# Two adaLN layers on one core: the first square weights are fetched inside layer 1's timetable, in the room of the softmax weights, and the tile for unread products has one buffer

## The chip, the core and the metric

The kernel runs on one core of a Trainium2 chip. A core has five engines with their own instruction streams: TensorE (PE in the profile; PEld is its weight load), VectorE (DVE), ScalarE (ACT), GpSimd (POOL) and SyncE (SP), which here only issues transfers. GpSimd issues transfers too. The engines wait for one another by semaphores. The metric is the time of one execution on the device, in microseconds; each figure is the median of several.

## The reference

Eight images of 512 tokens with 256 features pass through two layers. Each layer adds a modulated attention and a modulated feed-forward to its input (`ga`, `gb`, `ca`, ... come from a small product of a conditioning vector):

```python
def two_layers(x):
    h = _layernorm(x) * (1 + ca) + sa                  # layer 0
    x = x + ga * attn0(h)
    h = _layernorm(x) * (1 + cb) + sb
    x = x + gb * ffn0(h)
    h = _layernorm(x) * (1 + ca) + sa                  # layer 1, with its own mod
    x = x + ga * attn1(h)
    h = _layernorm(x) * (1 + cb) + sb
    return x + gb * ffn1(h)

def attn0(x):   # rmsnorm, 16 heads of 16; linear attention and a window of 64 tokens, side by side
    lin = linear_attention_causal(taylor_feature_map(q @ Wqf), taylor_feature_map(k @ Wkf), v)
    win = sliding_window_attention(q, k, v)
    return x + concatenate([lin, win]) @ Wout

def attn1(x):   # 16 heads of 16, rotary, causal softmax
    attn = softmax(where(causal, Q @ K.T * scale, NEG_INF))
    return (attn @ V) @ w_proj + b_proj

def ffn1(x):    # ternary weights times a scale per output; hidden width 1024
    h = silu(tlin(x, w1_w, w1_s)) * tlin(x, w2_w, w2_s)
    h = gelu(tlin(h, h1_w, h1_s), approximate=False)
    h = gelu(tlin(h, h2_w, h2_s), approximate=False)
    return tlin(h, w3_w, w3_s)
```

## The kernel before

**Layers 0 and 1 by a timetable.** Everything up to the first gates of layer 1's feed-forward is written as small functions that are put into one list `plan` with a time in steps: `when(t, f)` for layer 0, `when1(t, f)` for layer 1. The list is sorted by time, and the functions are called in that order under a manual schedule, so each engine's instructions stand in just this order. Layer 1's attention takes six steps for each of 32 units (an image, a half of the heads, one of two head sets), and layer 1's steps begin while layer 0 still runs.

**Maxima.** Both softmaxes subtract a maximum per query row. `scores` (layer 1) and `win_scores` (layer 0) multiply queries and keys into PSUM, and a `post` function runs a VectorE `tensor_tensor_reduce` over each block: it adds a mask, takes the minimum of the negated values, and leaves one number per row in `maxima` (L1128, L524). The instruction also writes its elementwise product. Nobody reads this: it goes to a tile `junk`, 512 bf16 wide, tagged `junk` with two buffers. The sums of squares of layer 0's norm (`squares`, L375) use the same tile. On VectorE each of these is two instructions: the reduction itself and a reading of the accumulator, which writes `maxima`. The transposes L538 (layer 0) then bring the maxima to the rows of the queries, where L544 adds them. L1225 transposes layer 1's result back to tokens, in a PSUM tag with two buffers (`mm`) that the projection out, whose sum with `x` is L1277, uses too.

**Room.** SBUF is given out in stacks from the left and from the right. On the left stand the pools `w0`, `tok0`, `fm0` and `at0`, opened in this order in one `lctx` that is closed at the end of the timetable. `at0` holds the softmax weights: the tag of each bank has 4, 3 or 2 buffers. Its last reader is the product `values` (L1209) of the last unit. On the right stand the feed-forward's weights `ffn_w` and, from step 187 on (`room`), its gates' parts `ffn_g`.

**The first gates.** Layer 1's feed-forward works on each image with hidden width 1024 in eight column blocks f. All its values are held as a high and a low part in a 32-bit format that TensorE takes faster (`split`: a VectorE cast L195 makes the high part, and L196 the low one, on GpSimd where `rest` says so). The first image's gates are part of the timetable: `gated(f)` at steps 200.0, 200.6, 203.7, 209.6, 211.0, 214.0, 215.0 and 216.0 multiplies (L1377), `gate_parts` follows with the Silu (L1389), the product (L1392, into `row`, a tag `flat` of two buffers) and the split, whose low part is GpSimd's for the first seven.

**The feed-forward.** After the timetable a flag is loaded on every engine, and a branch (L1547) takes one of two versions. The one that runs here, `feed_forward(True)`, opens its pools where `lctx` had been, in the order `h2`, `g2`, `tok2`, `hw`, `mm2`. Its first transfers on GpSimd's queue are the eight slices (512 KB each) of the first square matrix `h1T`, then eight of the second, `h2T`, then `w3T`. Inside the branch, instructions are ordered by a scheduler. The first square product is `times("h1T", ...)`, L1466, with row L1512 on ScalarE (Gelu) and a split; the second is the same line with L1518.

Of the kernel before, what the change touches and what calls it, by code (L numbers as in the profile page):

```python
# [8 lines left out]
FP = mybir.dt.float32  # L9
BF = mybir.dt.bfloat16  # L10
# [14 lines left out]
NF = DH // P  # L25
WIN = 64
BIG = 3.0e38
PAD = (24, 32)

# [5 lines left out]
def adaln_two_layers_kernel(ctx: ExitStack, tc: tile.TileContext, t, out):  # L37
# [163 lines left out]
    with ExitStack() as lctx:  # L201
        wp = lctx.enter_context(tc.tile_pool(name="w0", bufs=1))
        tok = lctx.enter_context(tc.tile_pool(name="tok0", bufs=1))
        fm = lctx.enter_context(tc.tile_pool(name="fm0", bufs=1))
        atp = lctx.enter_context(tc.tile_pool(name="at0", bufs=2))
        sc = lctx.enter_context(tc.tile_pool(name="sc0", bufs=3, space=PSUM))
        mm = lctx.enter_context(tc.tile_pool(name="mm0", bufs=2, space=PSUM))
        only0 = ExitStack()
# [74 lines left out]
        def when1(time, what):  # L283
            slow = min(max(time, 0.0), END1)
            plan.append((20 * B + 0.6 + slow + STEP1 * (time - slow), len(plan), what))
# [49 lines left out]
        def prepare(b):  # L335
# [35 lines left out]
            def squares(j):  # L371
                if j == 0:
                    rms["ss"] = tok.tile([P, NTB], FP, name="ss", tag="ss", bufs=2)
                junk = tok.tile([P, T], BF, name="junk", tag="junk", bufs=2)[:, :D]
                nc.vector.tensor_tensor_reduce(  # L375
                    junk, ln["x"][:, j, :], ln["x"][:, j, :], 1.0 / D, 0.0, ALU.mult, ALU.add, rms["ss"][:, j : j + 1]
                )
# [124 lines left out]
        def win_scores(m, h, p, ps):  # L502

            q, k = ready[m // 2, m % 2, "q"], ready[m // 2, m % 2, "k"]
            mats, posts = [], []
            for ii in range(4):
                for i in range(2):
                    for e in range(2):
                        r = slice(64 * p + 32 * i, 64 * p + 32 * i + 32)
                        blk = 4 * h + ii  # L510
                        k0 = max(blk - 1, 0) * 64
                        mats.append(
                            lambda i=i, e=e, ii=ii, r=r, blk=blk, k0=k0: nc.tensor.matmul(  # L513
                                ps[64 * e : 64 * e + 64, i, ii * P : (ii + 1) * P],
                                q[r, e, 64 * blk : 64 * blk + 64], k[r, e, k0 : k0 + P],
                                start=True, stop=True,
                            )
                        )
                for i in range(2):

                    def post(i=i, ii=ii, blk=4 * h + ii):
                        junk = tok.tile([P, T], BF, name="junk", tag="junk", bufs=2)[:, :P]
                        col = 64 * p + 32 * i + 16
                        nc.vector.tensor_tensor_reduce(  # L524
                            junk, ps[:, i, ii * P : (ii + 1) * P], wmask[:, int(blk > 0), :], -1.0, BIG,
                            ALU.add, ALU.min, maxima[:, blk, col : col + 1],
                        )

                    posts.append(post)
            return mats, posts  # L530
# [335 lines left out]
        def bring(i):  # L866
            if i == 0:
                got1["wqkv"] = wp.tile([P, NC, 3 * D], FP, name="wqkv", tag="wqkv")
                nc.sync.dma_start(out=got1["wqkv"], in_=t["L1_attn_w_qkv"].rearrange("(k p) n -> p k n", p=P))
            elif i == 1:  # L870
                got1["rope"] = fm.tile([P, 2, T], FP, name="rope", tag="qm", bufs=2)
                nc.sync.dma_start(out=got1["rope"][:, 0, :], in_=t["rope_cos"])
                nc.sync.dma_start(out=got1["rope"][:, 1, :], in_=t["rope_sin"])
            elif i == 2:


                cmask = got1["cmask"] = fm.tile([P, T], FP, name="cmask", tag="cat0", bufs=2)
                nc.gpsimd.memset(cmask, 0.0)
                diag = cmask[:, T - P : T]
                nc.gpsimd.affine_select(  # L880
                    out=diag, in_=diag, pattern=[[-1, P]], compare_op=ALU.is_ge, fill=-4e9, base=0, channel_multiplier=1
                )
            elif i == 3:

                home = [rp.tile([P, 2, T], FP, name="home", tag="aw", bufs=4) for _ in range(2)]
                got1["wproj"], wps[0] = (home[0][:, i, :].rearrange("p (k n) -> p k n", k=NC) for i in range(2))
                got1["bproj"], got1["bc"] = (home[1][:, 0, i * D : (i + 1) * D] for i in range(2))
                nc.sync.dma_start(out=got1["wproj"], in_=w_proj)
                nc.sync.dma_start(out=got1["bproj"], in_=t["L1_attn_b_proj"].partition_broadcast(P))
                nc.sync.dma_start(out=got1["bc"], in_=mod_dram[0, 4, :].partition_broadcast(P))  # L890
            else:
                only0.close()
                fpool = got1["ffn"] = ctx.enter_context(tc.tile_pool(name="ffn_w", bufs=1, side="right"))
                lp = got1["lp"] = only1.enter_context(tc.tile_pool(name="only1", bufs=1, side="right"))
                got1["wproj"] = load(lp, "wproj", [P, NC, D], w_proj)
                got1["bproj"] = load(lp, "bproj", [P, D], t["L1_attn_b_proj"].partition_broadcast(P))

                for name in ("w1T", "w2T"):
                    full[name] = fpool.tile([P, NC, DH], FR, name=name, tag=name)
                full["h"] = [fpool.tile([P, NC, T], FR, name="h" + e, tag="h" + e) for e in "hl"]  # L900

                fpool.tile([P, PAD[0]], FP, name="pad0", tag="pad0")
                for name in ("w1_s_cols", "w2_s_cols", "h1_s_cols", "h2_s_cols"):
                    full[name] = load(fpool, name, [P, NF], t[name])
                full["w3_s"] = load(fpool, "w3_s", [P, D], t["L1_ffn_w3_s"].partition_broadcast(P))
                full["x0"] = fpool.tile([P, NTB, D], FP, name="x0", tag="x0")
                full["low"] = fpool.tile([P, 22], FP, name="low", tag="low")
                full["flag"] = fpool.tile([1, 1], I32, name="flag", tag="flag")
# [195 lines left out]
        def scores(n, step):  # L1104
# [6 lines left out]
            for qb in ((3,), (2,), (1, 0))[bank]:  # L1111
                m = (qb + 1) * P
                for i, g in enumerate(gs):
# [10 lines left out]

                    def post(i=i, g=g, qb=qb, m=m, o=o):
                        col = 32 * g + 16
                        junk = tok.tile([P, T], BF, name="junk", tag="junk", bufs=2)
                        nc.vector.tensor_tensor_reduce(  # L1128
                            junk[:, :m],
                            ps[:, i, o : o + m],  # L1130
                            got1["cmask"][:, T - m :],
                            -1.0,
                            BIG,
                            ALU.add,
                            ALU.min,
                            maxima[:, NTB * e + qb, col : col + 1],
                        )
# [247 lines left out]
        def gate_parts(f, i):  # L1385
# [4 lines left out]
            else:  # L1390
# [3 lines left out]
                )  # L1394
                split([part[:, f, :] for part in full["g"]], row, nc.gpsimd if f < NF - 1 else None)

        when1(187.0, room)
        for f, at in enumerate((200.0, 200.6, 203.7, 209.6, 211.0, 214.0, 215.0, 216.0)):
            when1(at, lambda f=f: gated(f))
            for i in range(2):  # L1400
                when1(at + (0.3, 0.35)[i], lambda f=f, i=i: gate_parts(f, i))
# [6 lines left out]
    def feed_forward(exact):  # L1408
# [3 lines left out]
        with ExitStack() as fctx:  # L1412
# [3 lines left out]
                w3 = h2p.tile([P, NF, D], FR, name="w3", tag="w3")  # L1416
            gp = fctx.enter_context(tc.tile_pool(name=f"g2{exact}", bufs=1 if exact else 2))
            tok = fctx.enter_context(tc.tile_pool(name=f"tok2{exact}", bufs=2 if exact else 1))
            if exact:
                tok.tile([P, PAD[1]], FP, name="pad1", tag="pad1", bufs=1)  # L1420
            hp = fctx.enter_context(tc.tile_pool(name=f"hw{exact}", bufs=1 if exact else 3))
            mm = fctx.enter_context(tc.tile_pool(name=f"mm2{exact}", bufs=8, space=PSUM))

            if exact:
                h1 = hp.tile([P, NF, DH], FR, name="h1", tag="h1")
                for dst, name in ((h1, "h1T"), (h2, "h2T")):
                    src = t[name].rearrange("(k p) n -> p k n", p=P)
                    for k in range(NF):
                        nc.gpsimd.dma_start(out=dst[:, k, :], in_=src[:, k, :])
                nc.gpsimd.dma_start(out=w3, in_=t["w3T"].rearrange("(k p) n -> p k n", p=P))  # L1430
                full.update(h1T=h1, h2T=h2)

                gs = [full["g"], [gp.tile([P, NF, T], FR, name="g" + e, tag="g" + e) for e in "hl"]]
                xs = [full["x0"], tok.tile([P, NTB, D], FP, name="x1", tag="x1", bufs=1)]
# [184 lines left out]
```

## Time and profile before

| | us |
|---|---|
| median of 3 runs | 1836.17 |
| the runs | 1834.57 to 1839.29 |
| the profiled execution | 1837.94 |
| its span | 1836.2 |
| layer 1's attention at its densest | about 800 to 1155 on the span's scale |
| last product of the timetable's gates (L1377) starts | 1182.60 |
| first product of the square weights (L1466) starts | 1189.72 |

The span is counted from the first to the last instruction of the profiled execution; 1.74 us of that execution lie around it. All places in time below are on the span's scale. In the profile's group lines, the figures behind the bar are busy time, the mean duration of one instruction in ns, and the idle time of the engine in front of the group with what ended most of it. In lines of the timeline they are the start, the duration and, in brackets, idle time before and what ended it. In lines of windows, each engine's busy time with its instructions stands in the order PE, PEld, DVE, ACT, POOL, and then the granted TensorE clock (1.00 is full speed), the share of the DMA engines and GB/s.

### The profile page before, as it was taken

To read this page: it belongs to the slowest core of one execution; us is meant where nothing else is said; L and a number is where in the kernel's file an instruction comes from. 1 tells how busy PE (TensorE), PEld (TensorE's weight loads), DVE (VectorE), ACT (ScalarE), POOL (GpSimd) and SP (SyncE) were. 2 spreads that over 40 slices of the span, in tenths; PEclk is the share of its full clock that TensorE was granted. 3 is DMA by queue.
4 is the path that set the end of the run, shared out by engine and by line. 5 is a ranking of instruction groups with operands and counts; after the bars stand their busy time and mean duration, and the time that the engine had idled before them with its cause. 6 is when DMAs were issued, how large, how long until landed. Compare 5 with 4: busy or idle time off the path is not lost.

```text
span 1836.2 us, 41129 instructions
## 1 busy us (share of the span) xinstructions
PE 1750.3 (95%) x16878; PEld 1196.4 (65%) x16878; DVE 1069.4 (58%) x3708; ACT 887.1 (48%) x1278; POOL 726.3 (40%) x1101
## 2 busy tenths in 40 slices
PE   3999999999999988999999999899999999999998
PEld 2456666666666655455455555588888888888887
DVE  3554665757566466578888887426353554636352
ACT  1675766667666644656666665323131322313221
POOL 4565857667575664357655555400000000000000
PEclk6899999999999999999999999999999999999999
DMA  4100011010100101022221110240000000000000
GB/s 150 45 2 14 5 39 37 5 37 5 40 17 17 57 4 39 1 65 93 72 61 61 62 47 27 100 148 26 1 26 7 21 26 1 27 1 26 1 12 14
DMA packets 41894, 65.98 MB, mean 36 GB/s; under 512 B 4057, under 2 KB 33369, under 8 KB 41697
## 3 DMA queue, kind: packets, MB, share of 16 engines
q1 hardware_dynamic: 36512, 47.02, 8.1%
q0 software_dynamic: 5184, 16.25, 2.9%
q8 instruction: 134, 2.20, 0.5%
q14 instruction: 64, 0.52, 0.1%
HBM read 50.63 MB, written 12.63 MB: 34 GB/s over the span
## 4 chain that ended last, share of the span: by engine, by line
PE 81%; ACT 8%; POOL 5%; issue 2%; DVE 2%; DMA 1%; SPq 0%; POOLq 0%; ACTq 0%; DVEq 0%
PE mm L1466 31%; PE sc L1175 7%; PE mm L717 5%; PE mm L166 4%; PE mm L620 4%; PE sc L480 4%; PE mm L1209 4%; PE mm L1529 3%; PE mm L1027 2%; PE sc L557 2%; PE mm L1267 2%; ACT at L491 2%; PE mm L643 2%; PE mm L1085 2%; PE mm L445 2%
## 5 line engine op out<-in xcount | busy, mean ns | idle before, releaser
L1466 PE MATMUL mm<-gh,h 128*128 128x512 f32 x1024 | 398.8, 391 | 6.7 <-issue 6.7
L1466 PE MATMUL mm<-gl,h 128*128 128x512 f32 x1024 | 398.0, 391 | 0.0
L1128 DVE CUSTOM_DVE_ANT_0 junk<-sc,cmask 128x256 bf16<-128x256 f32 (+3 forms) x512 | 225.0, 486 | 93.2 <-PE sc L1117 92.8
L195 DVE CAST gh<-row 128x512 fp32r<-128x512 f32 x192 | 80.6, 423 | 264.9 <-ACT row L1512 128.9
L1186 ACT ACTIVATE at<-sc 128x768 f32<-128x768 f32 (+1 forms) x192 | 168.7, 881 | 116.0 <-PE sc L1117 102.8
L1466 PEld LDWEIGHTS mm<-gh,h 128*128 128x128 f32 x1024 | 193.3, 189 | 47.3 <-issue 7.1
L1466 PEld LDWEIGHTS mm<-gl,h 128*128 128x128 f32 x1024 | 193.1, 189 | 40.0
L577 POOL TENSOR_SCALAR_AFFINE_SELECT aw<-aw 64x512 f32<-64x512 f32 (+1 forms) x320 | 168.1, 552 | 101.4 <-ACT aw L567 95.5
L491 ACT ACTIVATE at<-sc 128x768 f32<-128x768 f32 (+1 forms) x192 | 164.0, 883 | 68.7 <-PE sc L480 68.0
L1117 PE MATMUL sc<-k,q 32*128 32x512 f32 (+3 forms) x1024 | 192.0, 472 | 3.4 <-ACT at L1186 3.4
L1175 PE MATMUL sc<-qs,k 32*128 32x384 f32 (+3 forms) x1024 | 189.8, 470 | 1.7 <-DVE qs L1159 1.7
L1190 POOL TENSOR_SCALAR_AFFINE_SELECT at<-at 128x256 f32<-128x256 f32 x256 | 103.1, 415 | 187.5 <-ACT at L1186 187.2
L524 DVE CUSTOM_DVE_ANT_0 junk<-sc,wmask 128x128 bf16<-128x128 f32 x512 | 115.2, 285 | 83.6 <-PE sc L513 83.4
L495 POOL TENSOR_SCALAR_AFFINE_SELECT at<-at 128x256 f32<-128x256 f32 x256 | 103.7, 426 | 105.6 <-ACT at L491 104.7
L1518 ACT ACTIVATE row<-mm,h_s_cols 128x512 f32<-128x512 f32 x64 | 44.0, 687 | 194.5 <-PE mm L1466 194.5
L196 DVE TENSOR_TENSOR gl<-row,gh 128x512 fp32r<-128x512 f32 x185 | 126.7, 688 | 7.2
L1175 PEld LDWEIGHTS sc<-qs,k 32*128 32x128 f32 x1024 | 81.5, 184 | 68.4 <-DVE maxima L1128 35.4
L1512 ACT ACTIVATE row<-mm,h_s_cols 128x512 f32<-128x512 f32 x64 | 43.8, 688 | 153.2 <-PE mm L1466 153.1
L480 PE MATMUL sc<-qm,qk 32*128 32x512 f32 (+3 forms) x1024 | 101.8, 475 | 1.1 <-ACT at L491 0.6
L1117 PEld LDWEIGHTS sc<-k,q 32*128 32x128 f32 x1024 | 82.8, 185 | 12.2 <-ACT at L1186 8.0
L1506 ACT ACTIVATE sg<-mm,w_s_cols 128x512 f32<-128x512 f32 x56 | 38.6, 690 | 103.5 <-PE mm L1466 94.5
L567 ACT ACTIVATE aw<-sc 128x1024 f32<-128x1024 f32 (+1 forms) x64 | 62.2, 972 | 43.3 <-PE sc L557 38.7
(232 smaller groups left out, 3535.7 us busy)
## 6 DMA issues: line engine op xcount, KB each, us to landing
x_mid<-x SPq DMA_DIRECT2D x16, 512.0 KB, 3.2
x<-x_mid POOLq DMA_DIRECT2D x9, 512.0 KB, 4.4
x<-in_L_attn_x_dram SPq DMA_DIRECT2D x8, 512.0 KB, 4.0
raw<-in_h1T_dram SPq DMA_DIRECT2D x8, 512.0 KB, 3.4
raw<-in_h2T_dram SPq DMA_DIRECT2D x8, 512.0 KB, 3.4
h<-in_h1T_dram POOLq DMA_DIRECT2D x8, 512.0 KB, 7.1
h<-in_h2T_dram POOLq DMA_DIRECT2D x8, 512.0 KB, 10.9
out_dram<-tmp SPq DMA_DIRECT2D x16, 256.0 KB, 2.1
```

The lines of the kernel that those rows point to most:

```text
L196: (rest or nc.vector).tensor_tensor(parts[1], src, parts[0].bitcast(FP), ALU.subtract)
L480: lambda i=i, r=r, kb=kb, n=n, o=o: nc.tensor.matmul(ps[:, i, o : o + n], k[r, e, kb * P : (kb + 1) * P], qm[r, e, kb * P : T], start=True ...
L491: nc.scalar.activation(at, ps[:, :, :o], AF.Square, scale=0.5)
L495: nc.gpsimd.affine_select(out=d, in_=d, pattern=[[0, 2], [1, P]], compare_op=ALU.is_ge, fill=0.0, base=0, channel_multiplier=-1,)
L524: nc.vector.tensor_tensor_reduce(junk, ps[:, i, ii * P : (ii + 1) * P], wmask[:, int(blk > 0), :], -1.0, BIG, ALU.add, ALU.min, maxima[:, ...
L577: nc.gpsimd.affine_select(out=d, in_=d, pattern=[[0, d.shape[1]], [sign, 64]], compare_op=ALU.is_ge, fill=0.0, base=0, channel_multiplier= ...
L1117: nc.tensor.matmul(ps[:, i, o : o + m], q[r, e, qb * P : (qb + 1) * P], k[r, e, :m], start=True, stop=True,)
L1128: nc.vector.tensor_tensor_reduce(junk[:, :m], ps[:, i, o : o + m], got1["cmask"][:, T - m :], -1.0, BIG, ALU.add, ALU.min, maxima[:, NTB * ...
L1175: nc.tensor.matmul(ps[:, i, o : o + m], k[r, e, kb * P : (kb + 1) * P], qs[r, kb * P : T], start=True, stop=True)
L1186: nc.scalar.activation(at, ps[:, :, :o], AF.Exp, scale=0.25)
L1190: nc.gpsimd.affine_select(out=d, in_=d, pattern=[[0, 2], [1, P]], compare_op=ALU.is_ge, fill=0.0, base=0, channel_multiplier=-1,)
L1466: nc.tensor.matmul(ps, w[:, k, col : col + P], part[:, k, :], start=(k == 0 and i == 0), stop=(k == n - 1 and i == len(parts) - 1),)
```

## The change

There are three edits.

1. `junk` has one buffer in place of two, in all three places.
2. `at0` gets an exit stack of its own. A new function `first_large`, at step 201.5 of layer 1's timetable, closes it, opens a pool `ffn_h` on the right side for the first square matrix, and issues its eight transfers on GpSimd there. The feed-forward's own pool for it goes, and only `h2T` and `w3T` are fetched in the branch.
3. The padding tile of `tok2` goes, and the constant of paddings with it.

In the order of instructions on GpSimd the eight transfers now stand behind the low parts (L196) of the first two gates and in front of the other five. On TensorE the order differs in the first square product alone: before, the products of column blocks 0 to 2 were interleaved as slices of the weights came in, and after, each block runs through its eight slices in turn. On ScalarE the first Gelu now stands in front of the square root of L145, and one more table load goes with that.

```diff
-PAD = (24, 32)
...
-        atp = lctx.enter_context(tc.tile_pool(name="at0", bufs=2))
+        atctx = ExitStack()
+        atp = atctx.enter_context(tc.tile_pool(name="at0", bufs=2))
...
-                junk = tok.tile([P, T], BF, name="junk", tag="junk", bufs=2)[:, :D]
+                junk = tok.tile([P, T], BF, name="junk", tag="junk", bufs=1)[:, :D]
...
-                        junk = tok.tile([P, T], BF, name="junk", tag="junk", bufs=2)[:, :P]
+                        junk = tok.tile([P, T], BF, name="junk", tag="junk", bufs=1)[:, :P]
...
-                fpool.tile([P, PAD[0]], FP, name="pad0", tag="pad0")
+                fpool.tile([P, 24], FP, name="pad", tag="pad")
...
-                        junk = tok.tile([P, T], BF, name="junk", tag="junk", bufs=2)
+                        junk = tok.tile([P, T], BF, name="junk", tag="junk", bufs=1)
...
+        def first_large():
+
+            atctx.close()
+            hpool = ctx.enter_context(tc.tile_pool(name="ffn_h", bufs=1, side="right"))
+            h1 = full["h1T"] = hpool.tile([P, NF, DH], FR, name="h1", tag="h1")
+            for k in range(NF):
+                nc.gpsimd.dma_start(out=h1[:, k, :], in_=t["h1T"].rearrange("(k p) n -> p k n", p=P)[:, k, :])
+
         when1(187.0, room)
+        when1(201.5, first_large)
...
             if exact:
-                tok.tile([P, PAD[1]], FP, name="pad1", tag="pad1", bufs=1)
-            hp = fctx.enter_context(tc.tile_pool(name=f"hw{exact}", bufs=1 if exact else 3))
-            mm = fctx.enter_context(tc.tile_pool(name=f"mm2{exact}", bufs=8, space=PSUM))
-
-            if exact:
-                h1 = hp.tile([P, NF, DH], FR, name="h1", tag="h1")
-                for dst, name in ((h1, "h1T"), (h2, "h2T")):
-                    src = t[name].rearrange("(k p) n -> p k n", p=P)
-                    for k in range(NF):
-                        nc.gpsimd.dma_start(out=dst[:, k, :], in_=src[:, k, :])
+                for k in range(NF):
+                    nc.gpsimd.dma_start(out=h2[:, k, :], in_=t["h2T"].rearrange("(k p) n -> p k n", p=P)[:, k, :])
                 nc.gpsimd.dma_start(out=w3, in_=t["w3T"].rearrange("(k p) n -> p k n", p=P))
-                full.update(h1T=h1, h2T=h2)
+                full["h2T"] = h2
```

More of the change, by code (lines that the diff above doesn't have):

```diff
@@ L1418, in feed_forward @@
             tok = fctx.enter_context(tc.tile_pool(name=f"tok2{exact}", bufs=2 if exact else 1))
-            if exact:
-                tok.tile([P, PAD[1]], FP, name="pad1", tag="pad1", bufs=1)
-            hp = fctx.enter_context(tc.tile_pool(name=f"hw{exact}", bufs=1 if exact else 3))
+            if not exact:
+                hp = fctx.enter_context(tc.tile_pool(name="hw", bufs=3))
             mm = fctx.enter_context(tc.tile_pool(name=f"mm2{exact}", bufs=8, space=PSUM))
             if exact:
-                h1 = hp.tile([P, NF, DH], FR, name="h1", tag="h1")
-                for dst, name in ((h1, "h1T"), (h2, "h2T")):
-                    src = t[name].rearrange("(k p) n -> p k n", p=P)
-                    for k in range(NF):
-                        nc.gpsimd.dma_start(out=dst[:, k, :], in_=src[:, k, :])
+                for k in range(NF):
+                    nc.gpsimd.dma_start(out=h2[:, k, :], in_=t["h2T"].rearrange("(k p) n -> p k n", p=P)[:, k, :])
                 nc.gpsimd.dma_start(out=w3, in_=t["w3T"].rearrange("(k p) n -> p k n", p=P))
-                full.update(h1T=h1, h2T=h2)
+                full["h2T"] = h2
                 gs = [full["g"], [gp.tile([P, NF, T], FR, name="g" + e, tag="g" + e) for e in "hl"]]
```

## The prediction

> **What bounds the kernel now.** I read the page first: the busy shares, then the costliest groups with the idle time in front of each.
>
> ```profile
> span 1836.2 us, 41129 instructions
> ...
> PE 1750.3 (95%) x16878; PEld 1196.4 (65%) x16878; DVE 1069.4 (58%) x3708; ACT 887.1 (48%) x1278; POOL 726.3 (40%) x1101
> ...
> L1466 PE MATMUL mm<-gh,h 128*128 128x512 f32 x1024 | 398.8, 391 | 6.7 <-issue 6.7
> ...
> L1128 DVE CUSTOM_DVE_ANT_0 junk<-sc,cmask 128x256 bf16<-128x256 f32 (+3 forms) x512 | 225.0, 486 | 93.2 <-PE sc L1117 92.8
> ...
> L524 DVE CUSTOM_DVE_ANT_0 junk<-sc,wmask 128x128 bf16<-128x128 f32 x512 | 115.2, 285 | 83.6 <-PE sc L513 83.4
> ```
>
> TensorE sets the end: 95% busy, 86 us idle in all. Anything saved counts only where TensorE stands still, and anything added counts only where it makes TensorE stand still. The largest stop in the feed-forward is the 6.7 us before its first L1466. The two maxima groups, which the single junk buffer touches, wait for TensorE (93 and 84 us), so on average VectorE has room.
>
> Next, the order of time around that stop, and the landing times of the transfers of L1429.
>
> ```profile
> 1182.60 0.39 PE L1377 MATMUL sc<-hl,w2T 128*128 128x512 f32 x1
> ...
> 1183.82 0.75 DVE L1392 SCALAR_TENSOR_TENSOR row<-sc,w_s_cols,sg 128x512 f32<-128x512 f32 x1 [0.60 <-ACT sg L1389]
> ...
> 1184.88 4.31 POOL L1429 DMA_DIRECT2D h<-in_h1T_dram  x8 [0.33 <-DVE row L1392]
> ...
> 1189.72 0.77 PE L1466 MATMUL mm<-gh,h 128*128 128x512 f32 x1 [6.73 <-issue]
> ```
>
> ```profile
> DMA to landing us min/median/max: 4.5/10.3/10.9
> ```
>
> The gates' last product ends at 1182.99. GpSimd issues the first square weights at 1184.88, and the quickest landing, 4.5 us, puts the first at about 1189.4; TensorE starts 0.3 us later. "issue" means that the profile names no releaser; I take the landing, because the times fit.
>
> **The change, part by part.**
>
> *Early fetch.* In the new code the weights' eight transfers are issued behind the second gate's low part on GpSimd, about 1169.5 (1168.16 + 1.29), when the last reader of the softmax weights (L1209, ending 1164.06) is done. With the same 4.5 us they begin to land at 1174, and were the eight as far apart as in the old trace (1189.42 to 1199.31) the last would be there by 1184, before its turn. The first L1466 then waits for the next latest thing, the last gate's row, which ends at 1184.57. With the same 0.3 us behind the releaser it starts at 1184.87: 4.85 us earlier. The low parts of the last gate (VectorE, to 1185.76) are needed only after 14 matmuls, 3.1 us at 5.46 / 25 = 0.22 us each (a row further down), and are no new wait.
>
> The clock, by the windows' granted column:
>
> ```profile
> 1189.72:1195.19 5.47, 5.47 (x13) 4.29 (x14) 1.56 (x5) 0.57 (x2) 2.49 (x5) 0.50 1.13 417
> 1195.19:1200.65 5.46, 5.46 (x25) 4.49 (x25) 0.00 (x0) 0.00 (x0) 1.74 (x4) 1.00 1.13 408
> ```
>
> ```profile
> 730.98:734.39 3.41, 3.41 (x24) 0.74 (x20) 3.17 (x12) 1.58 (x3) 0.92 (x1) 0.50 0.02 5
> ```
>
> After the 6.73 us stop TensorE works 5.47 us at half clock, 13 matmuls where 25 fit next: 2.74 us lost. The new stop is 1184.87 − 1182.99 = 1.9 us. Two stops of that size exist: 1.70 us before 730.61 was followed by 3.41 us at 0.50, and 1.60 us before 142.14 by 6.83 us; three of 1.1 to 1.2 us were followed by none. I take the middle of the first two, 5.12 us, so 2.56 lost: gain 0.2, with bounds −0.7 (6.83 us) and +2.7 (none). Together **−5.0 us**, bounds −4.1 and −7.6. The Trainium skill ("TensorE: Matmul & The Clock Gate", section on HAM oscillation) asks only that idle gaps stay under some 3.4 us; by it the new stop would keep full clock and the term would be −7.6. The 1.70 us stop above, followed by half clock, speaks against it.
>
> *What the fetch passes on GpSimd.* Eight issues take 4.31 us, so the third gate's low part moves from 1171.99 to about 1173.8, and ends at 1175.1. Its row buffer is one of two; the fifth gate's row wants it at 1175.71. The cover is 0.6 us; without it the gates slip by at most one low part, 1.3 us, on VectorE, and TensorE feels it only through the last row. The following low parts (1174.28, 1177.00) are back in time by the second. SyncE's queue is not passed. The second square weights no longer stand behind the first, so they land earlier. The changed matmul order of the first block, a table load more on ScalarE (1.28 us), the removed padding and the lower addresses cost nothing that a row shows. The table load's cover is ScalarE's wait for TensorE, 2.8 us per row of that product (153.1 us over 55 at L1512); without it, 1.28 us.
>
> *One junk buffer.* Each reduction writes a junk tile that nobody reads, then a second instruction reads the accumulator. With two buffers a reduction overwrote the junk of the one before last, long done. With one it must wait for the reduction just before it. Counting in program order, 809 reductions follow another directly: 24 at L375, 417 at L524, 368 at L1128. The price, from the VectorE timeline:
>
> ```profile
> 911.81 0.08 DVE L1128 DVE_READ_ACCUMULATOR2_ANT maxima<- 128x1 f32 x1
> 911.81 0.29 DVE L1128 CUSTOM_DVE_ANT_0 junk<-sc,cmask 128x128 bf16<-128x128 f32 x1
> 912.02 0.08 DVE L1128 DVE_READ_ACCUMULATOR2_ANT maxima<- 128x1 f32 x1
> ...
> 912.23 0.42 DVE L310 BATCH_NORM_STATS2 st<-x 128x6 f32<-128x256 f32 x1
> 912.69 0.18 DVE L311 BATCH_NORM_AGGREGATE mv<-st 128x2 f32<-128x6 f32 x1
> ```
>
> Now a reduction starts together with the accumulator reading in front of it, 0.083 us before that ends. An instruction that needs its VectorE predecessor (L311 behind L310) starts about 0.034 us after its end. So each new wait costs 0.117 us, and VectorE gets 809 × 0.117 = 94.7 us of added time. The Trainium skill ("VectorE: DVE Perf Modes", section The DRAIN you can't avoid) reports that a semaphore after each of eight copies added nothing over one after the last. By it this term is 0 and the sum 1831.2; no run here shows such copies, and the rows above differ from it by 0.117 us a pair.
>
> How much reaches TensorE? The windows (TensorE's busy time is the first figure, VectorE's the third):
>
> ```profile
> 640.00:800.00 160.00, 145.99 (x1392) 82.78 (x1388) 97.37 (x364) 81.68 (x124) 82.47 (x119) 0.95 0.07 19
> 900.00:1000.00 100.00, 98.15 (x850) 49.73 (x849) 86.72 (x316) 65.82 (x94) 58.57 (x88) 1.00 0.20 62
> ```
>
> Layer 0 and the first stretch of layer 1 leave VectorE idle 40% of the time. From 800 to 1155 it is idle 12 to 19%, and gets 33.7 us of the new waits, 9.2 of them between 900 and 1000 where 13.3 are free. So bursts decide. I followed the tightest one, once per image (55.84 us) of layer 1. From 911.11 to 927.03 VectorE hardly stops. The burst of four at 911 makes 3 waits (0.35); the idle 0.16 before 913.03 takes back as much, leaving 0.19. Seven waits follow (0.82): 1.01. The idle 0.23 before 925.23 leaves 0.78; three more waits (0.35) make the sum of L1277, which ends at 927.03, 1.13 late. TensorE's transposes L1225 load at 927.42 into the buffer that it frees: slack 0.39. So 0.74 us late per image, for the six images from 815 to 1095: 4.4 us. In layer 0 an image has two bursts of eight reductions ahead of the transposes L538, 7 waits or 0.82 us, and the two I followed had 0.24 and 0.60 us to spare: 0.82 − 0.42 = 0.40 each. The second burst finds TensorE already late by the first, so I count one per image, eight images: 3.2. Sum **+7.6 us**. Bounds: 0, if the late products are made up in the next pause; above, all of the 33.7 us of the dense stretch and the 17 × 0.82 = 14 of the 17 weight loads of L643 that waited for L544: +48.
>
> Sum against the profiled execution: 1836.2 + 7.6 − 5.0 = 1838.8 span, with 1.74 around it 1840.5, beside 1837.94. The median shown is 1.77 below that execution: 1836.17 + 2.6 = 1838.8. I say **1839**.
>
> **Rivals.** (A) The forecast: 1839, within 0.3% (5.5 us, about what a measurement of this kernel can tell from no change). Chance 0.42.
> (B) VectorE's pauses absorb all waits and only the stop is saved: 1836.2 − 5.0 = 1831.2, or 1828.6 if the clock stays full. For it: 176 us of waiting for TensorE in the two maxima groups. Against: the unbroken run above. Chance 0.18, of which 0.12 lies under 1830.7.
> (C) VectorE becomes the bound in layer 1's dense stretch, 800 to 1155. It decides if VectorE, busy 87% and with the waits 96%, cannot use its last idle slices because they come in the wrong places; then each further wait moves TensorE. With half of 33.7 on the path: 16.9 + 3.2 − 5.0 = +15, 1851; with all, 1868. Slower counts from 10.5 us reaching TensorE. For it: ScalarE's and GpSimd's steps hang on the same slots. Against: the loads of L1175 that the waits view gives to the maxima (35.4 us, 79) leave the matmuls themselves only 1.7 us idle. Chance 0.28.
> (D) The early fetch doesn't start L1466 earlier, since "issue" was something else there, as fetching the branch's code: 1836.2 + 7.6 = 1843.8. Against: VectorE is in the branch's code by 1186.3. Chance 0.12.
>
> **How the numbers follow.** Slower by over 0.3% (above 1841.7): C and D, 0.40. Faster (below 1830.7): 0.12 from B. The rest 0.48. The range 1829 to 1853 holds A, D, most of B and C with half its waits; left out are C's upper half and B at full clock.
>
> **What would show it.** Right: L1466 starts within 2 us of L1377's end; its weights are issued near 1169 on that scale; reductions start 0.034 us after the accumulator reading; VectorE's span per reduction in a burst is 0.117 longer; per image period 55.84 grows by some 0.7 in layer 1. Wrong: reductions still starting with the reading (B), a period longer by 2 us or more (C), a stop of 6 us still there (D).

## The result, and the profile after

| | before | after |
|---|---|---|
| median of 12 runs, us | 1836.08 | 1840.59 |
| lowest to highest, us | 1834.57 to 1841.52 | 1837.75 to 1845.30 |
| span of the profiled execution, us | 1836.2 | 1840.9 |
| VectorE busy, us | 1069.4 | 1135.7 |
| stop before the first product of the square weights, us | 6.73 | 1.78 |

The ratio is 1.0018, with a 95% interval of 1.0009 to 1.0026: 3.3 us slower (1.7 to 4.8). A later comparison gave 1.0026 (1.0014 to 1.0038). The forecast was 1839, 2.8 us over the median it started from.

The groups of the page after the change, with the line numbers of the new kernel (the square products are L1471 there, L1466 before):

```profile
span 1840.9 us, 41132 instructions
...
PE 1753.6 (95%) x16878; PEld 1192.1 (65%) x16878; DVE 1135.7 (62%) x3708; ACT 889.0 (48%) x1279; POOL 727.4 (40%) x1101
...
L1471 PE MATMUL mm<-gh,h 128*128 128x512 f32 x1024 | 398.2, 390 | 1.8 <-issue 1.8
...
L1128 DVE CUSTOM_DVE_ANT_0 junk<-sc,cmask 128x256 bf16<-128x256 f32 (+3 forms) x512 | 250.6, 489 | 81.7 <-PE sc L1117 69.0
...
L524 DVE CUSTOM_DVE_ANT_0 junk<-sc,wmask 128x128 bf16<-128x128 f32 x512 | 148.5, 290 | 87.2 <-PE sc L513 71.6
```

VectorE is busy 66 us longer, 59 of it in the two groups of maxima (25.6 and 33.3 us more), while the mean of one reduction has hardly moved (486 to 489 and 285 to 290 ns). What went is an overlap: before, a reduction started some 0.08 us before the one in front had ended (at 912.02, where the one in front ran from 911.81 for 0.29, in the prediction's rows), and now it doesn't. The stop of the square products fell from 6.7 to 1.8 us.

The timeline of VectorE in a burst of the changed kernel shows what lies between:

```profile
920.08 0.08 DVE L1128 DVE_READ_ACCUMULATOR2_ANT maxima<- 128x1 f32 x1
920.20 0.29 DVE L1128 CUSTOM_DVE_ANT_0 junk<-sc,cmask 128x128 bf16<-128x128 f32 x1
920.41 0.08 DVE L1128 DVE_READ_ACCUMULATOR2_ANT maxima<- 128x1 f32 x1
920.53 0.29 DVE L1128 CUSTOM_DVE_ANT_0 junk<-sc,cmask 128x128 bf16<-128x128 f32 x1
920.75 0.08 DVE L1128 DVE_READ_ACCUMULATOR2_ANT maxima<- 128x1 f32 x1
920.75 0.42 DVE L310 BATCH_NORM_STATS2 st<-x 128x6 f32<-128x256 f32 x1
```

Each reduction now starts 0.12 us after the start of the accumulator reading in front (920.08 to 920.20, 920.41 to 920.53). An instruction of another kind (L310) still starts together with the reading. So only the reductions wait, as worked out. In this trace 743 of the 809 reductions that follow another start within 0.05 us behind the end of its reading; the others start later. Before, none starts so: 763 start together with the reading.

The timeline around the stop, and the granted clock behind it (column PEclk of the windows, in front of the DMA share and GB/s; first GpSimd's row of the issues):

```profile
1182.00 4.32 POOL L1403 DMA_DIRECT2D h<-in_h1T_dram  x8
```

```profile
1195.21 0.39 PE L1377 MATMUL sc<-hl,w2T 128*128 128x512 f32 x1
...
1196.42 0.75 DVE L1392 SCALAR_TENSOR_TENSOR row<-sc,w_s_cols,sg 128x512 f32<-128x512 f32 x1 [0.60 <-ACT sg L1389]
...
1197.38 0.47 PE L1471 MATMUL mm<-gh,h 128*128 128x512 f32 x1 [1.78 <-issue]
```

```profile
1197.38:1202.85 5.47, 5.47 (x24) 4.53 (x25) 3.30 (x12) 1.40 (x2) 3.78 (x8) 1.00 0.79 251
1202.85:1208.31 5.46, 5.46 (x26) 4.53 (x25) 3.80 (x9) 4.12 (x5) 1.57 (x2) 1.00 1.10 395
```

The weights are issued 13 us before the last gate's product, and the first square product starts 0.2 us behind the end of the last gate's row (1197.17). The semaphore records of the two traces say what held TensorE, where the view says only "issue": before the change its wait for the first slice's transfer ended at 1189.45, 0.03 us after the last packet landed; after it, its wait for VectorE ended at 1197.22, 0.05 us behind that row. Behind it the clock is full at once: 24 products in the window in which the old kernel did 13.

### The profile page after: what moved, and what is told of

Its sections match the earlier page's. It is cut to its first block, busy times and chain, and to the rows that moved or that the text cites. A ratio compares the mean times of both kernels' runs of the same rounds, so it can differ in the third digit from the quotient of the medians.

```text
span 1840.9 us, 41132 instructions
## 1 busy us (share of the span) xinstructions
PE 1753.6 (95%) x16878; PEld 1192.1 (65%) x16878; DVE 1135.7 (62%) x3708; ACT 889.0 (48%) x1279; POOL 727.4 (40%) x1101
## 4 chain that ended last, share of the span: by engine, by line
PE 72%; DVE 15%; ACT 5%; POOL 4%; issue 3%; DMA 1%; DVEq 0%; SPq 0%; POOLq 0%; ACTq 0%
PE mm L1471 31%; PE sc L1175 5%; PE mm L717 5%; DVE junk L1128 4%; PE sc L480 3%; PE mm L1534 3%; PE mm L1209 3%; PE mm L620 3%; PE mm L165 2%; PE mm L1027 2%; DVE junk L524 2%; PE sc L557 2%; PE mm L643 2%; PE mm L445 1%; PE mm L1085 1%
## 5 line engine op out<-in xcount | busy, mean ns | idle before, releaser
L1471 PE MATMUL mm<-gh,h 128*128 128x512 f32 x1024 | 398.2, 390 | 1.8 <-issue 1.8
L1471 PE MATMUL mm<-gl,h 128*128 128x512 f32 x1024 | 397.5, 389 | 0.0
L1128 DVE CUSTOM_DVE_ANT_0 junk<-sc,cmask 128x256 bf16<-128x256 f32 (+3 forms) x512 | 250.6, 489 | 81.7 <-PE sc L1117 69.0
L1471 PEld LDWEIGHTS mm<-gh,h 128*128 128x128 f32 x1024 | 192.2, 188 | 41.9 <-issue 2.2
L1471 PEld LDWEIGHTS mm<-gl,h 128*128 128x128 f32 x1024 | 192.2, 188 | 39.7
L524 DVE CUSTOM_DVE_ANT_0 junk<-sc,wmask 128x128 bf16<-128x128 f32 x512 | 148.5, 290 | 87.2 <-PE sc L513 71.6
```

The costliest lines, as they stand in the source:

```text
L524: nc.vector.tensor_tensor_reduce(junk, ps[:, i, ii * P : (ii + 1) * P], wmask[:, int(blk > 0), :], -1.0, BIG, ALU.add, ALU.min, maxima[:, ...
L1128: nc.vector.tensor_tensor_reduce(junk[:, :m], ps[:, i, o : o + m], got1["cmask"][:, T - m :], -1.0, BIG, ALU.add, ALU.min, maxima[:, NTB * ...
L1471: nc.tensor.matmul(ps, w[:, k, col : col + P], part[:, k, :], start=(k == 0 and i == 0), stop=(k == n - 1 and i == len(parts) - 1),)
```

## Where the time went, instruction by instruction

TensorE's instructions up to the last gate stand in the same order in all the traces here, but for small products that change places with close neighbours, and the square products have the same count. So the start of one TensorE instruction can be compared between two traces. The table gives that start less its start in the kernel before, in us (medians over 16 us; the columns are places in the old trace). The rows below "changed kernel" are experiments that come further down; where the text says "by the rows", it means this table, in which each row is one profiled execution. Chance stalls and half-clock stretches move a row by 1 to 3 us in places, above all before 180, between 640 and 760 and around 1150.

```
                               180    640    760   1140   last gate   600th square product
changed kernel                 3.7    8.1    7.1   10.8     12.6          5.1
changed kernel, again          0.0    2.6    3.3    6.8      8.7          1.2
one junk buffer alone          3.2    6.5    7.0   10.5     10.9         10.2
one in layer 0               - 0.5    2.1    3.2    3.2      4.9          3.8
one in layer 1               - 0.1  - 0.1    1.0    4.5      6.4          5.1
early fetch, two buffers     - 0.9  - 0.6  - 1.4  - 1.4      0.3         -7.2
early fetch, again           - 0.1  - 0.7  - 0.4  - 0.3    - 0.3         -7.8
products written to PSUM       0.8   10.1   11.6   22.5     23.4         15.9
fetch, two narrow buffers    - 2.0  - 1.9  - 1.8    1.7      2.1         -5.4
the same, again                3.0    2.7    3.3    6.9      7.2         -0.3
the same waits, other room     0.4    0.5    1.6    5.1      7.0         -0.5
fetch and filled stop        - 2.4  - 2.1  - 2.6  - 2.6    - 2.6        -10.1
fetch at step 214.5          - 0.7  - 0.9  - 1.2  - 1.2    - 1.1          3.4
```

Three steps are nearly the same wherever they occur. From 760 to 1140 each kernel with one junk buffer in layer 1 loses 3.5 to 3.7 us, and each with two loses 0.1 at most (the kernel with products in PSUM is a case of its own). From the last gate to the 600th square product each kernel with the fetch at step 201.5 gains 7.5 us. Some of that belongs to the one old trace: the three experiments that keep the old fetch (one junk buffer alone, in layer 0, in layer 1) gain 0.7 to 1.3 there too, with stops of 6.3 to 6.4 us in place of 6.7 and 3.6 to 4.7 us at half clock behind them in place of 5.5. Beside these, the fetch is worth 6.2 to 6.8. From 180 to 640 one buffer in layer 0 loses 2.6 to 4.4, two lose −0.6 to 0.3.

Within layer 1 most of the loss falls at two places of TensorE in each image: in the changed kernel the difference steps from 8.14 to 8.42 at the L1151 of 916.37 and from 8.45 to 8.71 at the L1225 of 927.53, and alike 55.8 us later; the single buffer alone and the one in layer 1 have the same steps to within 0.01 us. The waits of TensorE and of its weight loads, between 800 and 1155 of the changed kernel's trace, name both (what waited, for what, us in total, times, longest), the first once, where elsewhere the view says "issue". Neither row is there before:

```profile
PE mm L1151 <- DVE rows L1236: 0.3, 1, 0.3
```

```profile
PEld mm L1225 <- DVE x L1277: 1.7, 5, 0.3
```

The transposes L1151 write into the tag `mm`, too, whose buffer the rows of L1236 free.

## The experiments

All times are compared with runs of the kernel before on the same chip.

**The single buffer alone.**

```diff
 (the kernel before, in all three places)
-junk = tok.tile([P, T], BF, name="junk", tag="junk", bufs=2)
+junk = tok.tile([P, T], BF, name="junk", tag="junk", bufs=1)
```

> The kernel before with one junk buffer in all three places and nothing else. Theory (each reduction that directly follows another waits for it, and the bursts reach TensorE): the trace of the changed kernel is 12.6 us behind at the last gate, of which some are chance stalls; I expect +8 to +11 us, a ratio of 1.004 to 1.006, and reductions that start 0.03 to 0.04 us after the accumulator reading. Rival (VectorE's pauses absorb the waits, and the slowdown comes from the fetch's place in GpSimd's queue): within 0.1% of the kernel before. Rival (VectorE becomes the bound in layer 1): +15 or more.

Measured: ratio 1.0050 (1.0032 to 1.0067), 9.2 us slower. This settles that the waits cost time by themselves. Both rivals fall: it isn't nothing, and it isn't 15.

**The early fetch with two buffers.**

```diff
 (the changed kernel, junk in all three places)
-junk = tok.tile([P, T], BF, name="junk", tag="junk", bufs=1)
+junk = tok.tile([P, T], BF, name="junk", tag="junk", bufs=2)
...
-wqk = wp.tile([P, P], FP, name="wqk", tag="wqk")
+wqk = rp.tile([P, P], FP, name="wqk", tag="wqk")
```

> The changed kernel with two junk buffers again; the 256 bytes that are then short come from a small weight tile of layer 0 (wqk, 512 bytes) that moves to the right side. Theory: no waits between reductions, TensorE's stop before the square weights falls from 6.7 to about 1.8 us, with full clock after it or some 3.4 us at half: 4.9 to 7.6 us faster than the kernel before, a ratio of 0.9959 to 0.9973. Rival (the fetch's place in GpSimd's queue delays the gates): a stop of 1.8 us, but the last gate later by 3 us or more against the kernel before, and a ratio of 0.999 or more.

Measured: ratio 0.9951 (0.9932 to 0.9970), 9.0 us faster. The stop was 1.79 us. From place 1160, ahead of the fetch, to the last gate TensorE's difference to the kernel before stays as it is (0.25 and 0.27 us), so the fetch's place in GpSimd's queue delays nothing that TensorE feels.

**One layer at a time.** In the kernel before, the maxima of layer 0 and its squares get a junk tag of their own; one tag has one buffer, the other two.

```diff
 (layer 0: L374 and L522; layer 1: L1127)
-junk = tok.tile([P, T], BF, name="junk", tag="junk", bufs=2)
+junk = tok.tile([P, D], BF, name="junk", tag="junk0", bufs=1)   # layer 0; 2 in the other kernel
...
-junk = tok.tile([P, T], BF, name="junk", tag="junk", bufs=2)
+junk = tok.tile([P, T], BF, name="junk", tag="junk", bufs=2)    # layer 1; 1 in the other kernel
```

> The kernel before with one junk buffer for layer 0 (L375 and L524) and two of its own for layer 1 (L1128). Theory by the prediction's sum: +3.2 us (ratio 1.0017). By the traces' difference at 620 us, with two chance stalls taken off: +5. Rival (VectorE as the bound of layer 1 alone): within 1 us of the kernel before.

> The kernel before with one junk buffer for layer 1 (L1128) and two of its own for layer 0. Theory by the prediction's sum: +4.4 us (ratio 1.0024), and 0.3 to 0.7 us more per image between 800 and 1155. The two halves together give what the single buffer gives in all three places. Rival (VectorE as the bound of layer 1): +12 us or more.

Measured: layer 0 1.0024 (1.0013 to 1.0036), 4.4 us; layer 1 1.0015 (1.0004 to 1.0027), 2.8 us. Both layers carry a part, and the two together, 7.2, lie within the single buffer's interval of 5.9 to 12.3. Per image of layer 1 the rows give 0.6 us, as expected.

**No tile for the products.**

```diff
 (the changed kernel)
-junk = tok.tile([P, T], BF, name="junk", tag="junk", bufs=1)
 nc.vector.tensor_tensor_reduce(
-    junk[:, :m],
+    ps[:, i, o : o + m],
     ps[:, i, o : o + m],
...
-junk = tok.tile([P, T], BF, name="junk", tag="junk", bufs=1)[:, :P]
+junk = ps[:, i, ii * P : (ii + 1) * P]
```

> The changed kernel, in which the reductions of both softmaxes (L524, L1128) write their unread products back over the scores that they read, in PSUM, in place of the junk tile; the squares keep the one junk buffer. Nothing is read after it there, so no reduction waits for the one before. Theory (the wait is what costs): as fast as the changed kernel with two buffers, 1829 to 1832 us, a ratio of 0.995 to 0.998, with reductions that start together with the accumulator reading in front, unless a 32-bit result in PSUM takes longer than a 16-bit one in SBUF (then the mean of the reductions, 486 and 285 ns before, rises). Rival (what costs is something else about the smaller tile, its address for one): 1840, as the changed kernel.

Measured: ratio 1.0111 (1.0094 to 1.0129), 20 us slower. Neither theory expected it. The timeline of VectorE tells why:

```profile
930.63 0.14 DVE L1127 DVE_READ_ACCUMULATOR2_ANT maxima<- 128x1 f32 x1
930.80 0.43 DVE L1127 CUSTOM_DVE_ANT_0 sc<-sc,cmask 128x256 f32<-128x256 f32 x1
931.15 0.14 DVE L1127 DVE_READ_ACCUMULATOR2_ANT maxima<- 128x1 f32 x1
931.33 0.30 DVE L1127 CUSTOM_DVE_ANT_0 sc<-sc,cmask 128x128 f32<-128x128 f32 x1
...
931.93 0.14 DVE L1127 DVE_READ_ACCUMULATOR2_ANT maxima<- 128x1 f32 x1
931.93 0.42 DVE L310 BATCH_NORM_STATS2 st<-x 128x6 f32<-128x256 f32 x1
```

The reductions still wait for the one in front, as they start 0.03 us after the reading's end and L310 doesn't. I put this down to their writing into one PSUM tile; it was not tried apart. And the reading itself takes 0.14 us in place of 0.08. So this became an experiment on the price: 0.17 us a pair where the changed kernel pays 0.12. The loss from 760 to 1140 went from 3.5 to 10.9 us, three times as much for one and a half times the price (the new place of the products came along with it). The windows show the room that was left (VectorE's busy time is the third figure; first the changed kernel, then this one):

```profile
900.00:1000.00 100.00, 98.30 (x858) 49.68 (x856) 88.95 (x305) 65.46 (x94) 56.90 (x86) 1.00 0.20 60
```

```profile
900.00:1000.00 100.00, 96.51 (x843) 49.43 (x841) 93.18 (x301) 66.47 (x96) 60.67 (x89) 1.00 0.18 55
```

**Two narrow buffers for layer 0.**

```diff
 (the changed kernel, layer 0's window maxima)
-junk = tok.tile([P, T], BF, name="junk", tag="junk", bufs=1)[:, :P]
+junk = tok.tile([P, P], BF, name="junk", tag="junk0", bufs=2)
```

> The changed kernel, in which layer 0's window maxima (L524, 128 wide) get two narrow junk buffers of their own (512 bytes together, which fit as it stands); layer 1's and the squares' stay with one of 1 KB. Theory: layer 0's waits are gone and layer 1's stay: the fetch's gain of 7.7 us in the spans and layer 1's loss of 3.5 give 1832 to 1834, a ratio of 0.997 to 0.999. Rival (layer 1's maxima carry the loss): 1838 to 1840. On the clock: the stop of about 1.8 us before the square weights was followed by full clock in two profiles; if that is a rule, so here and in the kernel with PSUM results; if it was chance, one of them shows 3.4 or 6.8 us at half clock after it.

Measured: ratio 1.0005 (0.9995 to 1.0014). That is a miss: by the rows' steps (7.5 gained, 3.5 lost) it should have been 0.9978. Its row in the table looks better than it was, as the execution profiled was the fastest of its eleven (1832.11, median 1835.98). It was tried again, beside a kernel with nearly the same waits in the room of the early fetch (`wqk` on the right, `junk0` of 256 columns with two buffers, one `junk` for layer 1; the 24 waits of the squares L375 go here, too):

```diff
 (the early fetch with two buffers)
-junk = tok.tile([P, T], BF, name="junk", tag="junk", bufs=2)
+junk = tok.tile([P, D], BF, name="junk", tag="junk0", bufs=2)   # layer 0, twice
...
-junk = tok.tile([P, T], BF, name="junk", tag="junk", bufs=2)
+junk = tok.tile([P, T], BF, name="junk", tag="junk", bufs=1)    # layer 1
```

> The kernel with two narrow junk buffers for layer 0 once more. By the rows (7.5 us less from the last gate on, 3.5 more in layer 1) its ratio should be 0.9978; the comparison gave 1.0005, with 0.9995 to 1.0014. Expected 0.997 to 0.999 if that comparison was unlucky, 1.000 if the rows of one profile leave out a loss.

> The same waits as the kernel before it (two buffers for layer 0's maxima, one for layer 1's), but in the room of the early fetch with two buffers (wqk on the right side, all other tiles at that kernel's places). Expected by the rows: ratio 0.9978, 3.5 us slower than the early fetch alone. If this gives 0.998 and the other 1.000, the places of the tiles matter; if both give the same, they don't.

Measured: 0.9994 (0.9982 to 1.0005) and 0.9989 (0.9977 to 1.0000). Their intervals overlap, so the places of the tiles are not shown to matter. With the fetch in place, layer 1's single buffer costs some 5 us (0.9989 beside 0.9960 below, on different chips; by the two intervals 2 to 8), which fits the 3.5 of the dense stretch and does not ask for it alone; the narrow buffers' 1.0005 and 0.9994 ask for 6 to 8. Of the rest, the rows show 0.4 us from 1140 to the last gate with one junk buffer in layer 1 and none with two, beside 1.5 to 1.7 us in each of the six profiles, of both kinds, that have a half-clock stretch of 3.41 us there. They also show a part at the start of layer 1: from 640 to 760 the kernels with one junk buffer there lost 0.5 to 1.1 us in five of seven profiles, though so did one of the five with two. Where the remainder falls stays open.

**The fetch's worth, on one chip.** The changed kernel and the early fetch with two buffers, once more:

> The changed kernel itself once more, so that it stands on one chip beside the next three, all compared with the same runs of the kernel before. So far: ratio 1.0018. Expected 1.001 to 1.003; half-clock stretches after its stop of 1.8 us before the square weights in none of the profiles so far.

> The early fetch with two junk buffers once more, on the same chip as the changed kernel. Open: what the fetch is worth. The single comparison gave -9 us; the changed kernel less the single buffer gave -6, the two narrow buffers less layer 1's part gave -2. By the spans' rows it is 4.9 us of the stop and 0 to 2.7 of the clock. Expected: ratio 0.9958 to 0.9973 to the kernel before, and 0.0045 to 0.0055 under the changed kernel (the single buffer alone: 0.0050). If it is 0.9985 or more, the first comparison was luck and something else takes back part of the fetch.

Measured: 1.0026 (1.0014 to 1.0038) and 0.9960 (0.9949 to 0.9972), 7.3 us faster than the kernel before (5.1 to 9.4), which holds the rows' 7.5 and 6.2 alike. The timeline of the latter:

```profile
1182.27 0.39 PE L1377 MATMUL sc<-hl,w2T 128*128 128x512 f32 x1
1184.44 0.47 PE L1471 MATMUL mm<-gh,h 128*128 128x512 f32 x1 [1.78 <-issue]
1184.75 0.39 PE L1471 MATMUL mm<-gl,h 128*128 128x512 f32 x1
1184.98 0.40 PE L1471 MATMUL mm<-gh,h 128*128 128x512 f32 x1
```

From the second product on they follow at 0.23 us: full clock.

**The stop filled with work.**

```diff
 (the early fetch with two buffers)
+def filled():
+    ps = mm.tile([P, T], FP, name="mm", tag="mm")
+    for i in range(7):
+        nc.tensor.matmul(ps, full["w2T"][:, 0, :P], full["h"][0][:, 0, :], start=(i == 0), stop=(i == 6))
+
+when1(217.0, filled)
```

> The early fetch with two junk buffers, and seven products that nobody reads behind the last gate's, 7 times 0.23 = 1.6 us, so that TensorE's stop of 1.8 us is filled with work and the first L1466 (same place in time) follows after 0.2 us. This adds work that leaves the results alone. If the stop of 1.8 us brings half clock in some executions (the prediction took 5.1 us of it, 2.6 lost), this is 1 to 2.6 us faster than the kernel without the products. If it brings none, the two are the same within 0.05%.

Measured: 0.9964 (0.9951 to 0.9976), the same as without (0.9960) within what the two intervals allow; a gain of 1 to 2 us is not excluded by them. The seven products fill the stop:

```profile
1180.27 1.75 PE L1408 MATMUL mm<-hh,w2T 128*128 128x512 f32 x7
1182.22 0.47 PE L1479 MATMUL mm<-gh,h 128*128 128x512 f32 x1 [0.20 <-PE mm L1408]
```

So the comparison of times shows no clock cost of the stop of 1.8 us; that there is none rests more on the granted clock, full behind this stop in all eight profiles that have it.

**The fetch later.**

```diff
 (the early fetch with two buffers)
-when1(201.5, first_large)
+when1(214.5, first_large)
```

> The early fetch with two junk buffers, but at step 214.5 in place of 201.5, behind the sixth gate's low part on GpSimd. The eight issues then start at about 1181 and end at 1185.4, the first landing comes at about 1185.5, and TensorE's stop is 2.5 to 3 us. Slices 1.28 us apart feed six products of 0.22 us each, so nothing starves behind. Expected: 1 us later than the early fetch by the stop, and 0 to 3.4 us more by half clock behind a longer stop: ratio 0.997 to 0.9985.

Measured: 1.0025 (1.0016 to 1.0034), 4.6 us slower than the kernel before and 12 slower than the fetch at 201.5. The timeline of TensorE, and the clock of that stretch:

```profile
1186.73 0.47 PE L1471 MATMUL mm<-gh,h 128*128 128x512 f32 x1 [4.88 <-DVE st L142]
1187.04 0.55 PE L1471 MATMUL mm<-gl,h 128*128 128x512 f32 x1
1188.99 0.80 PE L1471 MATMUL mm<-gh,h 128*128 128x512 f32 x1 [1.40 <-DMA h<-in_h1T_dram]
...
1192.00 0.80 PE L1471 MATMUL mm<-gh,h 128*128 128x512 f32 x1
1192.59 0.63 PE L1471 MATMUL mm<-gl,h 128*128 128x512 f32 x1
1193.27 0.79 PE L1471 MATMUL mm<-gh,h 128*128 128x512 f32 x1
```

```profile
1187.12:1200.77 13.65, 11.36 (x23) 5.83 (x22) 1.97 (x9) 2.19 (x3) 5.17 (x9) 0.50 1.12 391
```

My expectation missed three things. The first slice's last packet landed at 1186.43, 5.8 us after its issue and not 4.5, and TensorE's wait for it ended at 1186.46 (the bracket of the first row names VectorE's L142, which ended at about the same time). The first block takes its slices in turn, with two products for each slice and not six, so it goes at the pace of the landings, 1.28 us a slice (1192.00 to 1193.27); the kernel before had three blocks interleaved. And 13.65 us run at half clock. The fetch at step 201.5 doesn't meet this, because its slices are there before their turn: in the changed kernel the last is issued at 1185.7, and the longest landing takes 9.1 us, to 1194.8 at the latest.

## Why the prediction was right, point by point

- **The stop.** Predicted 4.85 us shorter, to 1.9; it is 4.95 shorter, 1.78. The first product waits for the last gate's row, as said, and before the change it waited for the landing.
- **The clock behind it.** This is the term that was mis-sized: 0.2 gained by the prediction, 2.6 by the rows (7.5 from the last gate to the 600th product, less 4.95), and 1.7 to 2.2 beside the three other traces with the old fetch. The mistaken step was to take the stops of 1.60 and 1.70 us elsewhere as the measure, and the middle of what followed them. Eight profiles have the stop of 1.8 us at this place, and in none is it followed by half clock. Full clock, the prediction's bound of −7.6, was what came. The Trainium skill ("TensorE: Matmul & The Clock Gate", section on HAM oscillation) asks that idle gaps stay under some 3.4 us; had the prediction gone by it, the term would have been right here. It doesn't fit the 1.70 us stop of the kernel before, behind which the granted clock was 0.50.
- **GpSimd's queue.** Predicted at nothing, with 0.6 us of cover. The third low part moved behind the eight issues, and the difference at the last gate is that of 20 us earlier (12.6 and 12.6). Right.
- **The price of a wait.** Predicted 0.117 us, measured 0.12. The Trainium skill ("VectorE: DVE Perf Modes", section The DRAIN you can't avoid) reports of eight copies that a semaphore after each costs nothing extra. That doesn't carry over to these pairs: the start of the second instruction moves by 0.12 us, and the single buffer alone cost 9.2 us. Without the wait these neighbours overlap, and the wait takes this overlap away and adds some 0.03 us.
- **What reaches TensorE.** Predicted 3.2 us in layer 0 and 4.4 in layer 1, 7.6 together. The rows give 2.6 to 4.4 between 180 and 640, 3.5 between 760 and 1140, and 0.4 from there to the last gate. The comparisons give 9.2 (5.9 to 12.3) for all three places at once and 7.2 for the two layers apart, so the term is about right, and that it was too small is not shown. In layer 1 the place was right and the split wrong: of the 0.74 us per image that were expected at L1225, 0.26 fall there, and 0.28 fall 11 us earlier at L1151, which waits for the rows of L1236; in all an image loses 0.62. I take it that a stop of TensorE at L1151 gives VectorE time to catch up, so the lateness doesn't pile up to the end of the run as I added it. Outside these stretches the start of layer 1 may cost, too. In the first 180 us, two of four profiles with one junk buffer in layer 0 are 3.2 and 3.7 us behind and two are not, but a kernel with two narrow buffers there is 3.0 behind as well in one profile and 2.0 ahead in the other: there, chance is as large as what is looked for.
- **The sum.** Forecast +7.6 and −5.0, measured apart +9.2 (7.2 by layers) and −7.3. The fetch's term was some 2 us too small, just outside the interval of 5.1 to 9.4; the waits' term may have been too small by as much. That the net came so near, 2.6 forecast and 1.9 from the parts, is partly luck, as the errors cancel; the changed kernel itself gave 3.3 and 4.8 in its two comparisons.
- **The rivals.** VectorE absorbing all waits (B) is refuted by the single buffer. VectorE as the bound of layer 1 (C) is not what happened, with 11 us idle between 900 and 1000 after the change and 0.62 us lost per image, but it was not far: at 0.17 us a pair 7 us are idle there, and the loss is threefold. A start that doesn't move (D) is refuted by the timeline.

The early fetch with two buffers beats both kernels: 0.9951 and 0.9960 of the kernel before. With the second buffer the room is 256 bytes per partition short, and a 512-byte weight tile of layer 0 that moves to the other side makes it up.

## What to carry to other kernels

A tile that nobody reads still orders the instructions that write it: with one buffer each writer waits for the one in front, and on an engine that goes in bursts some of that comes out at the next engine's tightest hand-over, long before the mean load is full. When a change has a saving and a price, measure them apart: a net of a few us was 9 lost and 7 gained, and 256 bytes were all that tied them together. A stop of TensorE in front of dense products can cost more than its length: behind the stops of 6.3 to 6.7 us here stood 3.6 to 5.5 us at half clock, behind those of 1.8 us none. So look at the granted clock of the first microseconds after it.

## What the runs showed of the hardware

- The reading of the accumulator takes 0.08 us behind a reduction that writes 16 bits to SBUF and 0.14 us behind one that writes 32 bits to PSUM, on the same scores; which of the two differences does it was not tried apart.
- The length of a stop alone does not tell whether half clock follows. A stop of 1.70 us at 728.9 in the kernel before was followed by it 0.4 us after work resumed; the 1.78 us stops before the square products never were; and behind one of 4.88 us, with starving products after it, stood 13.65 us. Even at one place it varies: each of the 14 profiles has a stop of 1.7 to 2.1 us between 726 and 742, and half clock begins within 0.6 us of the work's resumption in four, 6 to 7 us after it in seven, and not within 8 us in three.
